# One block in eight of the scan's input multiplied by a diagonal on TensorE instead of being scaled on ScalarE and transposed

## The chip, the cores and the metric

The kernel runs on one core of one Trainium2 chip. The metric is the time on the device, in microseconds (us), of one execution; the number given for a kernel is the median of several. A core has TensorE (PE in the profile; its weight loads are PEld), VectorE (DVE), ScalarE (ACT), GpSimd (POOL), and SyncE (SP), which here issues the DMAs.

## What is computed

The network has two layers on an input of 8 images of 64 x 64 pixels with 192 channels. Layer 0 is a state space block with convolutions and an MLP; the change does not touch it. Layer 1 is a selective scan over the pixels in four directions. Cut to what matters, with L = 4096 positions, 384 inner channels, 16 states and K = 4 directions:

```python
xs = four orders of the pixels                 # (b, K, 384, L)
delta = softplus(dts + bias)                   # (b, K, 384, L)
def step(h, inp):                              # one position
    d, bm, cm, uu = inp
    h = exp(d[..., None] * A) * h + (d * uu)[..., None] * bm[:, :, None, :]
    return h, einsum('bkdn,bkn->bkd', h, cm)   # h: (b, K, 384, 16)
_, ys = scan(step, h0, (delta, B, C, xs))
```

For every channel c and state n the state h obeys h(t) = e(t) h(t-1) + g(t), with e(t) = exp(delta(c,t) A(c,n)) and g(t) = delta(c,t) u(c,t) B(n,t). The output is the sum over the 16 states of C(n,t) h(t). The four directions are added up, normalised, gated and projected.

## The kernel before

**Layout.** Layer 0 runs first for all images. Then, image by image, a `front` (input projection and convolution) and, beside it, the `finish` of the image before; their order is worked out by a small planner. Then comes `main`, the scan of the image, in which every engine keeps the order in which the code writes its instructions (`keep_in_program_order`). The scan is nearly the whole of layer 1.

**Steps and units.** A step is a direction k (0 to 3) and a chunk of 512 positions: 32 steps for an image. A step has 8 pairs p of states and 3 blocks d of 128 channels, so 24 units, numbered u = 3p + d. A unit puts two states times 64 channels on the 128 partitions, and the two halves f of its 128 channels side by side, so its tiles are 128 x 2 x 512 in fp32.

**What a unit does**, in the order of `main`:

- `run(u)`: two scans on DVE (L1634), `hs` from `ea` and `g`, one per half f. POOL then copies the last column for the next chunk (`cy`, L1646) and multiplies by C (`hc`, L1648).
- `decay(u + 2)`: two exponentials on ACT, `ea` (L1607), into one of three buffers.
- `weigh`: ACT makes the input of the scan. `duT` holds delta times u with positions on the partitions, four blocks j of 128 positions by 384 channels. For a state n, `pw` is `duT[:, j]` times B(n), a number per partition (L1592): 384 elements. Two states i = 0, 1 fill one tile `pw` per p and j, so a pair takes 8 calls, spread over three units as 3, 3 and 2. They run ten calls ahead. There are eight buffers.
- `supply(u + 1)`: PE transposes `pw` block by block (L1618), eight transposes of 128 x 128 into `g` in PSUM, with channels and states on the partitions and positions along the free axis. `g` has two buffers.
- `collect(u - 1)`: PE adds the two states of `hc` into `y` (L1663), for each half f a fp32 matmul with 64 output columns onto partitions 0 to 63 or 64 to 127. In direction 0, the first pair also adds the skip term (`dskip`, L1661).
- `add(u - 2)`: after the last pair DVE adds `y` to the image's sum.
- pieces of `prepare(s + 1)`, one or a few at fixed units: the projections of the next step on PE (`p_d` L1481 at units 2 to 4, `p_b` L1497, `p_dt` L1510 at 7, 9 and 12, `p_du` L1532), softplus on ACT, and products on DVE. They share one PSUM bank.

So PE's order is: group of transposes for unit u + 1, `collect(u - 1)`, pieces, group of unit u + 2, and so on. `ident` is the 128 x 128 identity; `bt` holds B with positions on the partitions.

Of the kernel before, what the change touches and what calls it, by code (L numbers as in the profile page):

```python
# [8 lines left out]
F32 = mybir.dt.float32  # L9
AF = mybir.ActivationFunctionType  # L10
# [18 lines left out]
NB1 = TT // 128  # L29
# [155 lines left out]
def step(engine, weight, do, after=None, table=None):  # L185
    return engine, weight, do, after, table
# [846 lines left out]
def layer1(tc, consts, x1s, mv1, out, w_in, w_x, w_dt, w_out):  # L1033
    nc = tc.nc
    ident, grp, eps, p128 = consts
# [5 lines left out]
    with ExitStack() as ctx:  # L1041
# [37 lines left out]
        for m in range(2 * DT):  # L1079
            for ct in range(CT):  # L1080
# [4 lines left out]
                    start=ct == 0,  # L1085
                    stop=ct == 1,
# [4 lines left out]
        o = lambda ins: keeper[-1](ins)  # L1091
# [343 lines left out]
        def scan(xo):  # L1435
# [5 lines left out]
            pools, ready = {}, {}  # L1441

            def spool(name, bufs, **kw):
                pools[name] = cx.enter_context(tc.tile_pool(name=name, bufs=bufs, reuse_waits="tile", **kw))
# [3 lines left out]
            state = [dict() for _ in steps]  # L1448
# [127 lines left out]
            def load_c(s, p):  # L1576
                state[s]["cb", p] = cb = pools["bc1"].tile([128, TT], F32, name="cb")
                for i in range(2):
                    o(
                        nc.sync.dma_start(  # L1580
                            out=cb[i * 64 : i * 64 + 64], in_=state[s]["cd"][2 * p + i].partition_broadcast(64)
                        )
                    )

            def weigh(s, p, j, i):

                st = state[s]
                if i == 0:
                    st["pw", p, j] = pools["pw1"].tile([128, 2 * DT, 2, 64], F32, name="pw")
                n = 2 * p + i  # L1590
                o(
                    nc.scalar.activation(  # L1592
                        st["pw", p, j][:, :, i],
                        st["duT"][:, j].rearrange("p (g c) -> p g c", c=64),
                        AF.Copy,
                        scale=st["bt"][:, j, n : n + 1],
                    )
                )

            def decay(u):  # L1600
                s, p, d = units[u]
                k, c = steps[s]
                made["e", u] = ea = pools["e1"].tile([128, 2, TT], F32, name="ea")
                for f in range(2):
                    at = 2 * d + f
                    o(
                        nc.scalar.activation(  # L1607
                            ea[:, f], state[s]["dr", d][:, f], AF.Exp, scale=an[:, k, p, at : at + 1]
                        )
                    )  # L1610

            def supply(u):
                s, p, d = units[u]
                made["g", u] = g = pools["g1"].tile([128, 2, TT], F32, name="g")
                for f in range(2):
                    for j in range(NB1):
                        o(
                            nc.tensor.transpose(  # L1618
                                g[:, f, j * 128 : j * 128 + 128],
                                state[s]["pw", p, j][:, 2 * d + f].rearrange("p a b -> p (a b)"),  # L1620
                                ident,
                            )
                        )
# [57 lines left out]
            def prologue(f, mq, front_pools):  # L1681

                yield "wait", "front"
                front_pools.close()
                for name, n in (("pr1", 2), ("dr1", 4), ("pw1", 8), ("bc1", 3), ("e1", 3)):
                    spool(name, n)
                load_first = prepare(0, lambda name: mq.tile([128, TT], F32, name=name, tag="mm"))
                ready.update({fn.__name__: fn for at in sorted(load_first) for fn, *_ in load_first[at]})
                r = yield step("SP", 0.1, ready["load"])
                yield "take", "mm"  # L1690
                r += 3.5
                for d in range(DT):
                    r = yield step("PE", 0.95, lambda: ready["project"](d), r)
                r = yield step("DVE", 0.7, ready["keep"])
                f.give("mm", r)
                f.at["xd"] = r
                yield "take", "mm"
                yield step("PE", 0.6, ready["turn_b"])
                r = yield step("DVE", 0.2, ready["keep_b"])
                f.give("mm", r)  # L1700
                f.at["bt"] = r
                load_c(0, 0)
                for d in range(DT):
                    yield "wait", ("du", d)
                for t in todo[:10]:
                    yield step("ACT", 0.55, lambda: weigh(*t), f.free["ACT"])
                for u in range(2):
                    yield step("ACT", 1.35, lambda: decay(u), None, "explog")
# [19 lines left out]
            def main():  # L1728
                for name, n, kw in (("h1", 3, {}), ("y1", 1, dict(space=PSUM)), ("g1", 2, dict(space=PSUM))):
                    spool(name, n, **kw)  # L1730
                supply(0)
                rest = iter(todo[10:])
                nu = len(units)
                for u, (s, p, d) in enumerate(units):
                    if p == 0 and d == 0:
                        pieces = prepare(s + 1) if s + 1 < len(steps) else {}
                    s2, p2 = (s, p + 1) if p < NP1 - 1 else (s + 1, 0)
                    if s2 < len(steps) and d == 0:
                        load_c(s2, p2)
                    run(u)  # L1740
                    if u + 2 < nu:
                        decay(u + 2)
                    for _ in range((3, 3, 2)[d]):
                        if t := next(rest, None):
                            weigh(*t)
                    if u + 1 < nu:
                        supply(u + 1)
                    if u >= 1:
                        collect(u - 1)
                    if u >= 2:  # L1750
                        add(u - 2)
                    for f, *args in pieces.get(p * DT + d, ()):
                        f(*args)
                collect(nu - 1)
                add(nu - 2)
                add(nu - 1)
                cx.close()

            def chains(f, mq, front_pools):
                f.pool("tmp", 2)  # L1760
                return [prologue(f, mq, front_pools)] + [prologue_of(f, d) for d in range(DT)]
# [3 lines left out]
        for b in range(nb + 1):  # L1765

            f = Flow(tc, after=True)
            f.STAY = 0.0
            keeper.append(f.keep)
            mq_x, fr_x, fi_x = ExitStack(), ExitStack(), ExitStack()  # L1770
            mq = mq_x.enter_context(tc.tile_pool(name="mq1", bufs=5, space=PSUM, reuse_waits="tile"))
            f.pool("mm", 5)
            chains = []
            if b < nb:
                xo = [ddp.tile([128, DT, L], F32, name=f"xo{i}") for i in range(2)]
                xo.append(ddp.tile([L, DIN], F32, name="xo2"))
                chains += front(f, fr_x, mq, b, xo)
                prologue, main = scan(xo)
                chains += prologue(f, mq, fr_x)
            if b:  # L1780
                chains += finish(f, fi_x, mq, b - 1)
            for gen in chains:
                f.chain(gen)
            f.run()
            fi_x.close()
            mq_x.close()
            keeper.append(tc.keep_in_program_order)
            if b < nb:
                explog(tc)
                main()  # L1790
# [103 lines left out]
```

## Time and profile before

| | |
|---|---|
| time, median of 3 runs | 23752.58 us (23742.58 to 23754.5) |
| profiled execution, its own time | 23759.13 us |
| its span | 23757.4 us |
| PE matmuls busy | 21089.6 us |
| PE weight loads busy | 10279.5 us |
| DVE busy | 21274.2 us |
| ACT busy | 21040.0 us |
| POOL busy | 16067.4 us |
| scans, L1634 (both forms) | 13024.0 + 1763.7 us |
| `hc` on POOL, L1648 | 14592.9 us, 2375 ns each |
| `pw` on ACT, L1592 | 8874.1 us, 16384 of 601 ns |
| `ea` on ACT, L1607 | 8120.5 us, 12288 of 709 ns |
| transposes, L1618 | 6788.4 us, 49152 of 279 ns |
| `y` on PE, L1663 | 6624.0 us, 24576 of 617 ns |

How to read it: busy is the time in which an engine had an instruction under way, and the mean of one instruction is from its start to its end, so neighbours overlap; for a row of instructions, the distance from start to start counts. The profile has the whole program, layer 0 too, in which POOL is little used; the scan is read from windows of it. A wait is put down to the semaphore that came last by the profile, and this can name the wrong engine. A fp32 matmul shows as two records of the same size, a transpose as one.

### The profile page before, as it was taken

To read this page: it belongs to the slowest core of one execution; us is meant where nothing else is said; L and a number is where in the kernel's file an instruction comes from. 1 tells how busy PE (TensorE), PEld (TensorE's weight loads), DVE (VectorE), ACT (ScalarE), POOL (GpSimd) and SP (SyncE) were. 2 spreads that over 40 slices of the span, in tenths; PEclk is the share of its full clock that TensorE was granted. 3 is DMA by queue.
4 is the path that set the end of the run, shared out by engine and by line. 5 is a ranking of instruction groups with operands and counts; after the bars stand their busy time and mean duration, and the time that the engine had idled before them with its cause. 6 is when DMAs were issued, how large, how long until landed. Compare 5 with 4: busy or idle time off the path is not lost.

```text
span 23757.4 us, 313126 instructions
## 1 busy us (share of the span) xinstructions
PE 21089.6 (89%) x100804; PEld 10279.5 (43%) x100804; DVE 21274.2 (90%) x22093; ACT 21040.0 (89%) x37507; POOL 16067.4 (68%) x12871
## 2 busy tenths in 40 slices
PE   7999999978888888888888888888888888888888
PEld 4444444434444444444444444444444444444444
DVE  7888888779998999899989998999899989998998
ACT  5666766669998999899989998999899989998998
POOL 1111111149995999599959985998699769976997
PEclk8999999989999999999999999999999999999999
DMA  2111111133233323333233233323332233233332
GB/s 50 45 44 44 46 44 43 39 99 81 81 79 107 81 82 78 107 81 82 76 112 81 82 77 109 81 81 79 110 82 81 78 107 82 81 85 100 82 83 67
DMA packets 1368290, 1859.75 MB, mean 78 GB/s; under 512 B 268576, under 2 KB 697024, under 8 KB 1357440
## 3 DMA queue, kind: packets, MB, share of 16 engines
q1 hardware_dynamic: 1366656, 1839.73, 28.7%
q8 instruction: 810, 13.27, 0.2%
q14 instruction: 824, 6.75, 0.1%
HBM read 1225.98 MB, written 210.50 MB: 60 GB/s over the span
## 4 chain that ended last, share of the span: by engine, by line
POOL 43%; PE 24%; ACT 15%; DVE 7%; issue 6%; DMA 4%; SPq 1%; POOLq 0%; ACTq 0%; DVEq 0%
POOL hc L1648 40%; ACT pw L1592 6%; ACT ea L1607 6%; POOL cy L1646 3%; PE p_f L956 3%; DMA xc<-xo 2%; DVE xs L1202 2%; PE p_f L976 2%; PE p_x L448 2%; PE y L1663 2%; PE p_o L873 2%; PE p_y L790 1%; PE g L1618 1%; PE p_d L1481 1%; PE p_z L531 1%
## 5 line engine op out<-in xcount | busy, mean ns | idle before, releaser
L1648 POOL TENSOR_TENSOR hc<-hs,cb 128x1024 f32<-128x1024 f32 x6144 | 14592.9, 2375 | 12.0 <-POOL cy L1646 9.9
L1634 DVE TENSOR_TENSOR_SCAN hs<-ea,cy,g 128x512 f32<-128x512 f32 x10752 | 13024.0, 1262 | 608.6 <-PE g L1618 411.1
L1592 ACT ACTIVATE pw<-duT,bt 128x384 f32<-128x384 f32 x16384 | 8874.1, 601 | 20.2 <-DVE duT L1539 20.2
L1607 ACT ACTIVATE ea<-dr,an 128x512 f32<-128x512 f32 x12288 | 8120.5, 709 | 189.2 <-DVE hs L1634 170.8
L1663 PE MATMUL y<-hc,sel 128*64 128x512 f32 x24576 | 6624.0, 617 | 1841.3 <-POOL hc L1648 1819.2
L1618 PEld LDWEIGHTS g<-ident,pw 128*128 128x128 f32 x49152 | 5288.7, 141 | 4336.8 <-issue 2671.4
L1618 PE MATMUL g<-ident,pw 128*128 128x128 f32 x49152 | 6788.4, 279 | 60.1 <-ACT pw L1592 28.6
L1646 POOL COPY cy<-hs 128x2 f32<-128x2 f32 x6144 | 1164.2, 189 | 3373.5 <-DMA out_x<-xl 1733.8
L1663 PEld LDWEIGHTS y<-hc,sel 128*64 128x64 f32 x24576 | 1225.9, 134 | 3254.1 <-POOL hc L1648 3031.3
L1634 DVE TENSOR_TENSOR_SCAN hs<-ea,g 128x512 f32<-128x512 f32 x1536 | 1763.7, 1202 | 159.0 <-PE g L1618 115.6
L365 POOL TENSOR_TENSOR s<-xs 96x512 f32<-96x512 f32 x64 | 121.1, 1892 | 2033.7 <-DVE xs L343 1522.9
L1202 DVE SCALAR_TENSOR_TENSOR xs<-pad,p,xs 128x4096 f32<-128x4096 f32 x192 | 860.9, 4484 | 43.4 <-ACT xs L1192 36.2
L1510 PE MATMUL p_dt<-xdbl,wd 13*128 13x512 f32 x1536 | 857.2, 639 | 41.0 <-DVE de L1523 39.1
L365 POOL TENSOR_TENSOR s<-sq 96x512 f32<-96x512 f32 x128 | 211.6, 1653 | 964.1 <-ACT sq L378 899.8
L1481 PE MATMUL p_d<-xc,wx 128*44 128x512 f32 x1536 | 791.6, 598 | 22.6 <-DMA xc<-xo 22.0
L343 DVE SCALAR_TENSOR_TENSOR x<-xx,p,x 96x512 f32<-96x512 f32 x1024 | 785.2, 815 | 19.4 <-ACT x L332 19.4
L956 PE MATMUL p_f<-h,wf 96*128 96x512 f32 x1536 | 761.9, 632 | 24.4 <-ACT zs L550 14.0
L343 DVE SCALAR_TENSOR_TENSOR xs<-xin,p,xs 96x512 f32<-96x512 f32 x1024 | 749.3, 767 | 4.6 <-ACT xs L332 4.6
L976 PE MATMUL p_f<-m,wf 128*96 128x512 f32 x1536 | 692.9, 601 | 0.0
L1532 PEld LDWEIGHTS p_du<-ident,de 128*128 128x128 f32 x3072 | 323.5, 141 | 610.2 <-DVE de L1523 405.8
L448 PE MATMUL p_x<-h,wi 96*128 96x512 f32 x1024 | 544.5, 664 | 12.3 <-ACT h L405 11.1
L365 POOL TENSOR_TENSOR s<-x 96x512 f32<-96x512 f32 x64 | 96.2, 1502 | 626.3 <-DVE x L343 477.2
(202 smaller groups left out, 19557.2 us busy)
## 6 DMA issues: line engine op xcount, KB each, us to landing
cb<-cd SPq DMA_DIRECT2D x4096, 128.0 KB
dr<-de SPq DMA_DIRECT2D x3072, 128.0 KB
xc<-xo SPq DMA_DIRECT2D x256, 768.0 KB
e<-csd SPq DMA_DIRECT2D x256, 384.0 KB
xl<-x SPq DMA_DIRECT2D x256, 384.0 KB
ut<-xo SPq DMA_DIRECT2D x128, 768.0 KB
ut<-xo SPq DMA_DIRECT2D x256, 384.0 KB
xo<-xs SPq DMA_DIRECT2D x48, 1024.0 KB
```

What stands on the lines that cost most here:

```text
L343: nc.vector.scalar_tensor_tensor(im(out[:, ct]), tap(ct, j), w[:, ct, j : j + 1], im(out[:, ct]), ALU.mult, ALU.add)
L956: nc.tensor.matmul(ps, wf1[:, ct, mt * 128 : mt * 128 + 128], h[:, ct], start=ct == 0, stop=ct == 1)
L976: nc.tensor.matmul(ps[:CP], wf2[:, kt, ct * CP : ct * CP + CP], m[:, kt], start=kt == 0, stop=kt == 5)
L1202: nc.vector.scalar_tensor_tensor(xs, tap(j), kw[:, d, j : j + 1], xs, ALU.mult, ALU.add)
L1481: nc.tensor.matmul(st["p_d"][:44], wx[:, d, k], st["xc"][:, d], start=d == 0, stop=d == DT - 1)
L1592: nc.scalar.activation(st["pw", p, j][:, :, i], st["duT"][:, j].rearrange("p (g c) -> p g c", c=64), AF.Copy, scale=st["bt"][:, j, n : n + 1],
L1607: nc.scalar.activation(ea[:, f], state[s]["dr", d][:, f], AF.Exp, scale=an[:, k, p, at : at + 1])
L1618: nc.tensor.transpose(g[:, f, j * 128 : j * 128 + 128], state[s]["pw", p, j][:, 2 * d + f].rearrange("p a b -> p (a b)"), ident,)
L1634: nc.vector.tensor_tensor_scan(rev(h[:, f]), rev(ea[:, f]), rev(g[:, f]), 0.0 if first(s) else state[s - 1]["cy"][:, p, d, f : f + 1], ALU ...
L1646: o(nc.gpsimd.tensor_copy(st["cy"][:, p, d], h[:, :, last]))
L1648: o(nc.gpsimd.tensor_mul(hc, h, bc(st["cb", p], 1, [128, 2, TT])))
L1663: o(nc.tensor.matmul(y[half[f]], sel, hc[:, f], start=p == 0 and k > 0, stop=p == NP1 - 1))
```

## The change

In the odd pairs p, block j = 3 (the last of four) is made in another way. `weigh` no longer multiplies the 384 channels of `duT` by B(n). It writes B(n) on a diagonal: `bd[:, i]` is the identity times B(n), 128 elements per partition, one tile `bd` with both states, two buffers. `supply` then does not transpose this block. For each half f and each state i a matmul takes 64 channels of `duT` as weights and the diagonal as the moving operand, onto partitions 0 to 63 or 64 to 127 of `g`; the product with a diagonal scales each position by its B and turns the block at the same time. For an odd unit, two of eight transposes become four matmuls. The pool of `pw` tiles has seven buffers instead of eight, since two pairs now make seven such tiles.

```diff
+            def diagonal(p, j):
+                return p % 2 == 1 and j == NB1 - 1
+
             def weigh(s, p, j, i):
                 st = state[s]
+                if diagonal(p, j):
+                    if i == 0:
+                        st["bd", p, j] = pools["pw1"].tile([128, 2, 128], F32, name="bd", bufs=2)
+                    n = 2 * p + i
+                    o(nc.scalar.activation(st["bd", p, j][:, i], ident, AF.Copy, scale=st["bt"][:, j, n : n + 1]))
+                    return
                 if i == 0:
                     st["pw", p, j] = pools["pw1"].tile([128, 2 * DT, 2, 64], F32, name="pw")
...
             def supply(u):
...
                 for f in range(2):
                     for j in range(NB1):
+                        if diagonal(p, j):
+                            at = (2 * d + f) * 64
+                            for i in range(2):
+                                o(
+                                    nc.tensor.matmul(
+                                        g[i * 64 : i * 64 + 64, f, j * 128 : j * 128 + 128],
+                                        state[s]["duT"][:, j, at : at + 64],
+                                        state[s]["bd", p, j][:, i],
+                                        start=True,
+                                        stop=True,
+                                    )
+                                )
+                            continue
                         o(
                             nc.tensor.transpose(
...
-                for name, n in (("pr1", 2), ("dr1", 4), ("pw1", 8), ("bc1", 3), ("e1", 3)):
+                for name, n in (("pr1", 2), ("dr1", 4), ("pw1", 7), ("bc1", 3), ("e1", 3)):
```

## The prediction

> **What bounds the kernel now.** I read the busy shares first, then the busy time of one step of the scan, then who waited for whom, then the timeline of a few units. Units are numbered u = 3p + d inside a step (24 units), a step is one direction and one chunk of 512 tokens; 8 images x 32 steps = 256 steps.
>
> The page: busy shares, and the chain by engine.
> ```profile
> PE 21089.6 (89%) x100804; PEld 10279.5 (43%) x100804; DVE 21274.2 (90%) x22093; ACT 21040.0 (89%) x37507; POOL 16067.4 (68%) x12871
> POOL 43%; PE 24%; ACT 15%; DVE 7%; issue 6%; DMA 4%; SPq 1%; POOLq 0%; ACTq 0%; DVEq 0%
> ```
> Three engines are level, and the chain is mostly POOL and PE. Next, the busy times of two whole steps of one image, one of direction 1 and one of direction 0 (columns: length, then PE, PEld, DVE, ACT, POOL).
> ```profile
> 12851.09:12916.64 65.55, 57.79 (x318) 28.47 (x316) 63.19 (x60) 65.38 (x120) 59.89 (x49) 1.00 0.32 83
> 12256.83:12323.28 66.45, 60.12 (x330) 29.17 (x329) 63.10 (x60) 65.31 (x119) 59.91 (x49) 1.00 0.27 74
> ```
> ACT is busy 65.38 of 65.55 us, so it looks like the bound. But the second step has the same ACT work and takes 0.9 longer: something else can set the length. The waits over 1,700 us of one scan (us, times, longest):
> ```profile
> DVE hs L1634 <- PE g L1618: 53.7, 82, 1.3
> PE y L1663 <- POOL hc L1648: 184.8, 352, 1.1
> PE g L1618 <- ACT pw L1592: 2.3, 10, 0.3
> ACT ea L1607 <- DVE hs L1634: 5.1, 8, 1.1
> ```
> DVE waits for PE's `g`, PE for POOL's `hc`, POOL for DVE's scan; PE almost never stands still for ACT's `pw`; ACT's only waits are for DVE. The timeline of unit 9 shows the loop (start, length, engine, work, idle before):
> ```profile
> 12870.79 2.38 POOL L1648 TENSOR_TENSOR hc<-hs,cb 128x1024 f32<-128x1024 f32 x1
> 12873.22 1.08 PE L1663 MATMUL y<-hc,sel 128*64 128x512 f32 x4 [0.53 <-POOL hc L1648]
> 12874.23 1.12 PE L1510 MATMUL p_dt<-xdbl,wd 13*128 13x512 f32 x2
> 12875.28 1.09 PE L1618 MATMUL g<-ident,pw 128*128 128x128 f32 x8
> 12876.30 1.08 PE L1663 MATMUL y<-hc,sel 128*64 128x512 f32 x4
> 12877.31 1.09 PE L1618 MATMUL g<-ident,pw 128*128 128x128 f32 x8
> 12876.51 2.45 DVE L1634 TENSOR_TENSOR_SCAN hs<-ea,cy,g 128x512 f32<-128x512 f32 x2 [1.14 <-PE g L1618]
> ```
> `hc` of unit 6 ends at 12873.17; then PE runs without a gap: `y`, `p_dt`, the transposes of unit 9 (end 12876.37), and 0.14 later the scan starts. It waits for all eight transposes, as `g` is one tile. The same at units 4 and 5, of the direction 1 step and of the direction 0 step, where PE has the extra `dskip` matmuls:
> ```profile
> 12862.22 2.45 DVE L1634 TENSOR_TENSOR_SCAN hs<-ea,cy,g 128x512 f32<-128x512 f32 x2 [0.44 <-ACT pw L1592]
> 12865.16 2.45 DVE L1634 TENSOR_TENSOR_SCAN hs<-ea,cy,g 128x512 f32<-128x512 f32 x2 [0.49 <-PE g L1618]
> ...
> 12266.91 1.08 PE L1661 MATMUL y<-xc,dskip 128*64 128x512 f32 x4
> 12267.82 1.03 PE L1663 MATMUL y<-hc,sel 128*64 128x512 f32 x4
> 12269.63 1.09 PE L1618 MATMUL g<-ident,pw 128*128 128x128 f32 x8
> 12270.86 2.45 DVE L1634 TENSOR_TENSOR_SCAN hs<-ea,cy,g 128x512 f32<-128x512 f32 x2 [1.29 <-ACT ea L1607]
> ```
> The releasers "ACT" are wrong here: each of these scans starts 0.14 after its last transpose ends (12269.63 + 1.09 = 12270.72). The 0.9 us of extra PE work turns a wait of 0.49 into 1.29 and the step from 65.5 into 66.5. So the loop DVE, POOL, PE sets the pace; ACT runs beside it with 0.2 us to spare per step.
>
> **The skill.** "TensorEngine Tiling (Array Packing)", Key Properties: changing the tiling mode drains TensorE. The trace agrees: `y` (64 columns) to `p_d` (44 columns) takes 0.91 from start to start, `y` to `g` (128 columns) 1.01, so a change costs 0.10. "FP8 and Floating Point Precision", TensorE Precision Notes: true fp32 takes four passes. Here a 512-column fp32 matmul is two records of 0.43 (`p_d` x2 takes 0.95 with a drain), while a 128-column transpose is one record of 0.11. "ScalarE: Activation LUTs", What ACT_TABLE_LOAD costs: 0.833 ns per element. In the timeline three `pw` of 384 take 1.52 and two `ea` of 512 take 1.23, which is 0.108 per 128 elements; it agrees.
>
> **The change, part by part.** Per step, four odd pairs.
>
> ACT: 8 ACTIVATEs go from 384 elements (0.51) to 128 (0.51 - 0.22 = 0.29): 1.7 us less per step, 63.7 of work. Worth 1.7 x 256 = 440 us if ACT set the pace; by the reading above, about nothing.
>
> PE, in the 12 odd units of a step: 2 of 8 transposes go (2 x 0.11), and 4 matmuls of 64 x 128 columns come, each in two records. Like the two halves of `y`, the pair for i = 0, 1 writes different partition halves, and `y`'s four records go in two rounds, so I take two rounds of 0.107 per pair. The order per f is three transposes, then the pair: the mode changes three times more inside the group. A change costs 0.10 drain plus 0.05 for a weight load that nothing hides (eight transposes take 1.02 to the next `y`: 0.05 + 8 x 0.109 + 0.10). Before, from the first start: 0.05 + 7 x 0.109 = 0.82 to the last start. After: transposes 0.05 + 0.33 + 0.10 = 0.48, pair 0.05 + 0.21 + 0.10 = 0.36, transposes 0.48, pair 0.05 + 0.107 to its last round: 1.48. **The group ends 0.66 later.** The following `y` is in the pair's mode and saves one change, so PE's queue grows by 0.51. Bounds: with no cost of changes 2 x 0.214 - 2 x 0.109 = +0.21; with the two halves one after the other 0.66 + 2 x 0.214 = +1.09. No gain is possible, since two rounds are longer than one transpose. I take 0.66, because each term is a row of this trace.
>
> At nothing: `pw` keeps its reuse distance (8 tiles per two pairs before, 7 now), `bd`'s two buffers come round after four pairs. If that were wrong, ACT would wait, and it has 3 us to spare then. PE's wait for `pw` becomes one for `bd`, which ACT finishes earlier than before; behind it queue `collect` and the pieces of `prepare`, as now. No DMA, DVE or POOL instruction changes.
>
> Where 0.66 lands, walked along the timeline of the direction 1 step; slack is the time from a group's end to its scan, less 0.14. Unit 3 has 0.61: +0.05. Unit 4 has none: its group (12860.99 to 12862.08) ends at 12862.74, +0.66. PE is free for the next `y` 1.59 after the group's start, at 12862.58 instead of 12862.07; with 0.86 for `y` and 0.95 for `p_d` the group of unit 5 starts at 12864.39, lasts 1.75, and its scan starts at 12866.28 instead of 12865.16: +1.1, and all that follows in DVE's order with it. Unit 9, into which PE runs without a gap: 1.1 + 0.66, +1.8. Unit 10 has 0.9 of slack: still +1.8. Unit 11: group 9 (from 12876.40), `y`, group 10, `y`, `p_dt` and group 11 now run back to back, 1.59 + 0.96 + 1.59 + 0.96 + 1.05 + 1.75, to 12884.30, and the scan that started at 12881.85 starts at 12884.44: +2.6. Units 15 to 17 have slacks of 0.5 to 0.8, which hold 0.66 but for +0.1. Units 21 to 23 have none, but PE stands 0.36 before each `y`, which takes up most of the 0.51: +0.66, then +0.1 in all. Sum **+3.5 us per step**. In direction 0 the `dskip` matmuls of unit 1, which run now while PE waits for `hc`, find no such gap behind the longer group of unit 3: unit 4 +1.2 and unit 5 +1.7, so +4.1 for the step.
>
> Sum: 8 images x (8 x 4.1 + 24 x 3.5) = 934 us. Front, finish and layer 0 do not change. The profiled execution took 23759.1 (span 23757.4), so about 24,690; the median 23752.6 is 6 us lower, within rounding.
>
> **Rivals.**
> (1) ACT is the bound after all: 440 us less, 23,310. For it: 65.38 of 65.55 busy. Against: ACT itself waits for DVE, the direction 0 step is longer at equal ACT work, and after the change the group of transposes must fit where no slack is left. It decides from the point where the group gets no longer at all, since units 4, 5, 9 and 21 have no slack, and only if the last thing those scans wait for is ACT's. Chance 0.06.
> (2) Changes of mode cost little when weights are loaded ahead: +0.21 to +0.40 per group. The same walk gives 0.9 to 1.8 per step, 23,990 to 24,240. For it: PE can load weights early. Against: every change in the trace costs 0.10 or more. Chance 0.09.
> (3) The two halves do not overlap (+1.09): about 6.2 per step, 25,350. For it: 128 columns is short. Against: `y`'s rounds. Chance 0.05.
> (4) ACT's relief and PE's cost cancel, within 0.2%: 23,750. It needs both bounds to be loose; chance 0.02.
>
> **How the numbers follow.** The main case, +0.4 to +0.9 per group, has 0.78: 24,240 to 25,050. Its point is 24,690. Slack that PE finds in POOL's jitter, or in a cheaper change of mode, lowers it more easily than anything raises it, so the range for 8 in 10 reaches from 24,150 to 25,050; it takes in part of (2) and leaves (1), (3) and (4) out. Faster by over 0.2% (what a measurement of this kernel can tell from no change, 47 us): 0.06, from (1). Same: 0.02. Slower: 0.92.
>
> **What would show it.** In the changed profile: a row of `g<-bd,duT` matmuls with 128-column operands, two rounds about 0.11 apart, groups of an odd unit 1.7 to 1.8 long instead of 1.09; `pw` 14336 times and 2048 short ACTIVATEs of about 0.38; ACT's share falling, with ACT waiting about 5 us per step for the scan; DVE's wait for `g` rising from 2.4 to about 5.9 per step, with new waits at units 5, 9, 11 and 21. It is wrong if odd groups last under 1.4, or if a scan with a longer group starts no later than now, or if ACT stays without waits.

## The result and the profile after

The changed kernel takes 24,691 us (24,677 to 24,711) against 23,753 (23,743 to 23,755): ratio 1.0395, 95% interval 1.0382 to 1.0407. The prediction was 24,690. The scans of the eight images are 115 to 118 us longer each (in the mean 2100 before and 2217 after, from the first scan instruction to the last), which is 938 of the 941 us between the two spans; all that lies outside the scans is as it was, to 4 us.

The page of the changed kernel: busy shares, the chain by engine, and five of the costliest groups (busy, mean ns of one, then idle of the engine before them and its releaser).
```profile
PE 22618.6 (92%) x119236; PEld 10836.1 (44%) x119236; DVE 21326.1 (86%) x22093; ACT 20987.2 (85%) x37507; POOL 16135.7 (65%) x12871
POOL 41%; PE 30%; DVE 11%; issue 7%; ACT 6%; DMA 5%; SPq 0%; POOLq 0%; DVEq 0%; ACTq 0%
L1657 DVE TENSOR_TENSOR_SCAN hs<-ea,cy,g 128x512 f32<-128x512 f32 x10752 | 13062.3, 1263 | 1386.7 <-PE g L1631 1269.1
L1617 ACT ACTIVATE ea<-dr,an 128x512 f32<-128x512 f32 x12288 | 8183.9, 713 | 1144.5 <-DVE hs L1657 1050.5
L1641 PE MATMUL g<-ident,pw 128*128 128x128 f32 x43008 | 6673.3, 284 | 16.5 <-DVE hs L1657 12.5
L1631 PE MATMUL g<-bd,duT 128*64 128x128 f32 x24576 | 2701.3, 298 | 0.0
L1596 ACT ACTIVATE bd<-ident,bt 128x128 f32<-128x128 f32 x2048 | 696.2, 388 | 0.0
```
The work of DVE and POOL is the same; PE has 1,530 us more of it. The idle time of DVE before its scans went from 609 to 1,387 us, and what ends it is now the new matmul, L1631. ACT's idle time before `ea` went from 189 to 1,145 us: it waits for DVE.

The same two steps as before the change, one of direction 1 and one of direction 0 (length, then PE, PEld, DVE, ACT, POOL busy).
```profile
13316.37:13385.66 69.29, 63.65 (x390) 30.61 (x388) 63.50 (x60) 65.19 (x119) 60.32 (x49) 1.00 0.30 77
12687.14:12757.75 70.61, 66.19 (x402) 31.41 (x400) 63.43 (x61) 65.19 (x119) 60.24 (x49) 1.00 0.27 76
```
65.55 became 69.29 (+3.7), and 66.45 became 70.61 (+4.2). PE and its weight loads are busier; the other engines gain at most 0.4 us of busy time. The timeline of units 4 and 5 of the direction 1 step, PE and then DVE (start, length, work, idle before):
```profile
13325.31 1.02 PE L1481 MATMUL p_d<-xc,wx 128*44 128x512 f32 x2
13326.26 0.55 PE L1641 MATMUL g<-ident,pw 128*128 128x128 f32 x3
13326.74 0.44 PE L1631 MATMUL g<-bd,duT 128*64 128x128 f32 x4
13327.11 0.55 PE L1641 MATMUL g<-ident,pw 128*128 128x128 f32 x3
13327.58 0.44 PE L1631 MATMUL g<-bd,duT 128*64 128x128 f32 x4
13327.85 1.03 PE L1686 MATMUL y<-hc,sel 128*64 128x512 f32 x4
...
13328.17 2.45 DVE L1657 TENSOR_TENSOR_SCAN hs<-ea,cy,g 128x512 f32<-128x512 f32 x2 [1.01 <-PE g L1631]
13331.57 2.45 DVE L1657 TENSOR_TENSOR_SCAN hs<-ea,cy,g 128x512 f32<-128x512 f32 x2 [0.95 <-PE g L1631]
```
Read the starts: transposes 0.48, pair 0.37, transposes 0.47, pair 0.27 to the next `y`, 1.59 in all where it was 1.08. The last matmul ends at 13328.02, 1.76 after the group began, and the scan starts 0.15 later. The waits over 1,700 us of one scan (us, times, longest; from 12753 to 14453, so that no pause between two images is in it) have grown on DVE's and ACT's side:
```profile
DVE hs L1657 <- PE g L1631: 137.7, 123, 1.9
ACT ea L1617 <- DVE hs L1657: 91.0, 174, 1.9
PE y L1686 <- POOL hc L1671: 120.5, 247, 1.2
```
DVE's wait for PE was 53.7, ACT's for DVE 5.1, PE's for POOL 184.8: PE has used up part of its own waits and passed the rest on to DVE.

### The profile page after: what moved, and what is told of

The parts are those of the page before. It is cut to its first block, busy times and chain, and to the rows that moved or that the text cites. A ratio compares the mean times of both kernels' runs of the same rounds, so it can differ in the third digit from the quotient of the medians.

```text
span 24698.7 us, 349990 instructions
## 1 busy us (share of the span) xinstructions
PE 22618.6 (92%) x119236; PEld 10836.1 (44%) x119236; DVE 21326.1 (86%) x22093; ACT 20987.2 (85%) x37507; POOL 16135.7 (65%) x12871
## 4 chain that ended last, share of the span: by engine, by line
POOL 41%; PE 30%; DVE 11%; issue 7%; ACT 6%; DMA 5%; SPq 0%; POOLq 0%; DVEq 0%; ACTq 0%
POOL hc L1671 38%; DVE hs L1657 4%; PE y L1686 4%; PE g L1641 4%; POOL cy L1669 3%; PE p_f L956 2%; PE p_dt L1510 2%; ACT ea L1617 2%; DVE xs L1202 2%; PE g L1631 2%; DMA ut<-xo 2%; PE p_f L976 2%; PE p_x L448 2%; ACT pw L1602 2%; PE p_o L873 1%
## 5 line engine op out<-in xcount | busy, mean ns | idle before, releaser
L1602 ACT ACTIVATE pw<-duT,bt 128x384 f32<-128x384 f32 x14336 | 7843.0, 602 | 18.4 <-DVE duT L1539 18.4
L1686 PE MATMUL y<-hc,sel 128*64 128x512 f32 x24576 | 6514.9, 608 | 1304.7 <-POOL hc L1671 1249.6
L1641 PE MATMUL g<-ident,pw 128*128 128x128 f32 x43008 | 6673.3, 284 | 16.5 <-DVE hs L1657 12.5
L1641 PEld LDWEIGHTS g<-ident,pw 128*128 128x128 f32 x43008 | 4571.9, 141 | 4693.2 <-issue 2242.0
L1631 PE MATMUL g<-bd,duT 128*64 128x128 f32 x24576 | 2701.3, 298 | 0.0
L1686 PEld LDWEIGHTS y<-hc,sel 128*64 128x64 f32 x24576 | 1349.9, 135 | 2281.6 <-POOL hc L1671 2175.4
L1631 PEld LDWEIGHTS g<-bd,duT 128*64 128x64 f32 x24576 | 1216.7, 135 | 1029.9 <-issue 983.7
L1596 ACT ACTIVATE bd<-ident,bt 128x128 f32<-128x128 f32 x2048 | 696.2, 388 | 0.0
```

The costliest lines, as they stand in the source:

```text
L1602: nc.scalar.activation(st["pw", p, j][:, :, i], st["duT"][:, j].rearrange("p (g c) -> p g c", c=64), AF.Copy, scale=st["bt"][:, j, n : n + 1],
L1631: nc.tensor.matmul(g[i * 64 : i * 64 + 64, f, j * 128 : j * 128 + 128], state[s]["duT"][:, j, at : at + 64], state[s]["bd", p, j][:, i], s ...
L1641: nc.tensor.transpose(g[:, f, j * 128 : j * 128 + 128], state[s]["pw", p, j][:, 2 * d + f].rearrange("p a b -> p (a b)"), ident,)
L1686: o(nc.tensor.matmul(y[half[f]], sel, hc[:, f], start=p == 0 and k > 0, stop=p == NP1 - 1))
```

## The experiments

The theory: the loop DVE, POOL, PE sets the pace of the scan; a longer group on PE costs time where no slack stands before its scan; the group's length is two rounds per pair plus the changes of mode. (A round is the time of one record of a matmul, or of two that write different halves of the partitions side by side. Transposes write 128 columns, `y`, `p_d` and the diagonal's matmuls 64 or fewer; going from the one kind to the other is a change of mode.) The rivals: ACT is the bound; the loss has another source (the wait for the diagonal, the pool); changes of mode are free; a group costs the same wherever it stands. Each comparison below is with runs of the kernel before on the same chip (23,746 to 23,763 in the median).

### Each half of the change alone

`e1_act_only`: `weigh` as in the change, `supply` with eight transposes.
```diff
-                                state[s]["pw", p, j][:, 2 * d + f].rearrange("p a b -> p (a b)"),
+                                state[s]["pw", p, j - diagonal(p, j)][:, 2 * d + f].rearrange("p a b -> p (a b)"),
```


> The ScalarE half of the change alone: it writes the diagonal (128 elements) and not the 384, and TensorE makes eight transposes as before, with block 2 taken a second time in place of block 3 (so block 3 of odd pairs is left out of the computation). Loop theory (DVE, POOL, PE set the pace): no change, 23,700 to 23,760, with ACT now waiting 1.7 us per step more. Rival, ACT is the bound: 440 us less, 23,310.

`e2_pe_only`: `weigh` as before, `supply` as in the change with `ident` for `bd`, eight `pw` buffers.
```diff
-                                        state[s]["bd", p, j][:, i],
+                                        ident,
```


> The TensorE half alone: ScalarE makes all eight 384-element products of a pair as before, TensorE makes the four small matmuls with the plain identity as moving operand (so B is left out of block 3 of odd pairs). Loop theory: all of the loss is here, 24,650 to 24,730. Rival, part of the loss comes from the wait for the diagonal or the smaller pool: clearly below 24,690. Rival, ScalarE's relief gave something back in the changed kernel: up to 25,130.

Measured: `e1_act_only` 23,698, ratio 0.9975 (0.9964 to 0.9986). `e2_pe_only` 24,687, ratio 1.0388 (1.0372 to 1.0404). The whole loss is in the TensorE half, and neither the wait for `bd` nor the pool has a part in it: with them gone and with ACT's old work back, the time is that of the changed kernel. ACT's relief alone is worth 60 us and not 440 (2 us below the range that the theory gave; a small gain, but a real one). A direction 1 step of `e1_act_only`, and its waits over 1,700 us:
```profile
12887.00:12952.53 65.53, 57.38 (x318) 28.52 (x316) 63.18 (x61) 63.98 (x120) 59.97 (x49) 1.00 0.31 78
```
```profile
ACT ea L1617 <- DVE hs L1644: 32.1, 70, 1.1
```
ACT is busy 1.4 us less, and the step is as long as before to 0.02 us; ACT waits for DVE, 32.1 us instead of 5.1. Where the 60 us are, step by step from the two traces, whose spans differ by 55: the first step of each direction is 0.9 us shorter (32 such steps, 29 us in all), the other steps of direction 0 together 11 us, and the last step of each image 1.0 (8 us in all). The other 160 steps are equal; their sum differs by less than 1 us. A first step of direction 1, before and in `e1_act_only`:
```profile
12654.99:12720.02 65.03, 58.14 (x318) 28.42 (x316) 60.55 (x60) 64.93 (x119) 60.01 (x49) 1.00 0.30 77
12626.25:12690.34 64.09, 57.34 (x318) 28.46 (x316) 60.58 (x60) 62.98 (x118) 59.82 (x49) 1.00 0.31 77
```
In the first steps the scans are shorter (the form without `cy`, 1.20 instead of 1.26 us), and with less work of ACT the step gets shorter, as the steady ones do not: there ACT was the last. So the rival holds for about one step in eight. In direction 0 the gain is at unit 4, whose scan starts 0.15 earlier; its cause is open. The remaining 7 us lie ahead of the first scan; over the traces kept here that scan starts anywhere from 5,038 to 5,075 us, although layer 0 is the same in all of them, so this is no effect of the change.

### What makes the group longer

`e3_one_mode`: the kernel before, a full fp32 matmul instead of a transpose for block 3 of odd pairs.
```diff
+                        if p % 2 == 1 and j == NB1 - 1:
+                            o(nc.tensor.matmul(out, block, ident, start=True, stop=True))
+                        else:
+                            o(nc.tensor.transpose(out, block, ident))
```


> The kernel before, with block 3 of odd pairs turned by a full fp32 matmul with the identity (128 columns, two records) and not by a transpose: the second round is paid as in the change, but no mode changes. Theory with the terms of the prediction: +0.22 per group, by the walk +1.1 us per step, 24,045. Rival, the rounds are what costs and mode changes are free: as slow as the changed kernel, 24,690.

`e7_matmuls_last`: the changed kernel, with the blocks in the order T T T T T T M M.
```diff
-                for f in range(2):
-                    for j in range(NB1):
+                for f, j in sorted(((f, j) for f in range(2) for j in range(NB1)), key=lambda at: diagonal(p, at[1])):
```


> The changed kernel with the six transposes of an odd unit first and the four matmuls after them: one more mode change in the group instead of three. Theory: the group ends 0.36 later than before and not 0.66, PE's queue grows by 0.2: +1.6 us per step, 24,175. Rival, mode changes are free: 24,690, as the changed kernel.

Measured: `e3_one_mode` 24,009, ratio 1.0101 (1.0083 to 1.0119). `e7_matmuls_last` 24,144, ratio 1.0159 (1.0142 to 1.0175). PE's timeline at unit 4, first of `e3_one_mode` (L1620 are the matmuls, two records each), then of `e7_matmuls_last`:
```profile
13040.99 0.55 PE L1622 MATMUL g<-ident,pw 128*128 128x128 f32 x3
13041.37 0.39 PE L1620 MATMUL g<-ident,pw 128*128 128x128 f32 x2
13041.59 0.49 PE L1622 MATMUL g<-ident,pw 128*128 128x128 f32 x3
13041.92 0.39 PE L1620 MATMUL g<-ident,pw 128*128 128x128 f32 x2
13042.24 1.08 PE L1662 MATMUL y<-hc,sel 128*64 128x512 f32 x4
```
```profile
13065.30 0.88 PE L1641 MATMUL g<-ident,pw 128*128 128x128 f32 x6
13066.11 0.66 PE L1631 MATMUL g<-bd,duT 128*64 128x128 f32 x8
13066.59 1.03 PE L1686 MATMUL y<-hc,sel 128*64 128x512 f32 x4
```
In one mode, three transposes take 0.38 (after a change) and 0.33, the matmul between them 0.22, and the group 1.25 to the next `y`; where `y` followed at once, the eight transposes took 1.02. The 0.23 are the two extra records. With the matmuls together at the end there is one more change instead of three and the group takes 1.29; spread out it takes 1.59. Both kernels do as many rounds as the changed one, and are 680 and 550 us faster than it (36 and 31 us below what was expected of them). Of the loss of 938 us, some 250 are the second round. The 550 go with two of the three changes of mode, as `e7_matmuls_last` differs from the changed kernel in nothing but the order. The last 135 go with the third change or with the matmuls being half as wide; no run takes these two apart. Free changes of mode are ruled out.

### Where the group stands

The change in one pair only; `pw` with eight buffers.
```diff
-                return p % 2 == 1 and j == NB1 - 1
+                return p == 5 and j == NB1 - 1
```


> The change in pair 5 alone (units 15 to 17), a quarter of it, where the walk finds slack of 0.5 to 0.8 before each scan. Theory: the slack holds the 0.66, +0.1 to +0.2 us per step, 23,780 to 23,810. Rival, every group costs the same share of the loss, wherever it stands: a quarter of 938, 23,990.

The same with `p == 1`:

> The change in pair 1 alone (units 3 to 5), where units 4 and 5 have no slack and PE also does p_d. Theory: +1.15 us per step, +1.6 in direction 0, 24,075. Rival, the same share everywhere: 23,990.

Measured: `e4_pair5` 23,771, ratio 1.0009 (1.0003 to 1.0016). `e5_pair1` 24,046, ratio 1.0123 (1.0108 to 1.0139). The same three groups cost 25 us in one place and 300 in another (9 us below the expected range, and 29 below the expected point). In the trace of `e4_pair5` the scan of unit 17 starts 0.2 later than before, relative to its step, and no other adds to that; in `e5_pair1` the shift is 0.68 at unit 4, 1.14 at unit 5 and 1.13 at the end of the step (1.03, 1.55 and 1.54 in direction 0; medians over the steps of a direction but its first and last). The place decides. The 25 us are a balance: in directions 1 to 3 the steps but the first lose 35 us together, and the first steps gain 12, as they did in `e1_act_only`.

### Half of the wait taken away

`g` as two tiles, one for each half, in the same banks:
```diff
-                made["g", u] = g = pools["g1"].tile([128, 2, TT], F32, name="g")
+                made["g", u] = g = [pools["g1"].tile([128, TT], F32, name=f"g{f}") for f in range(2)]
```
On the kernel before:

> The kernel before with g as two tiles, one per half, so that the first scan of a unit waits for four transposes and not for eight (0.44 us earlier). Loop theory: DVE's stalls at units 4, 9 and 21 fall by 0.4 each; then ACT, 65.4 us of work in a step, is the next bound: 23,640 to 23,700, most of the gain in direction 0. Rival, ACT is the bound already: no change in directions 1 to 3 and in direction 0, 23,753.

On the changed kernel:

> The changed kernel with g as two tiles. The first half of an odd unit is then ready 0.84 us earlier than in the changed kernel, before the point of the kernel before, while PE's queue still carries 0.51 more per odd unit. Theory (wait and queue both count): most of the loss goes, a part stays where PE runs without a gap (units 5, 11), about +0.7 us per step, 23,850 to 23,980. Rival, only the wait for the end of the group counts: the stalls are gone and ACT's relief shows, 23,400 to 23,500.

Measured: `e6_before_two_tiles` 23,661, ratio 0.9966 (0.9953 to 0.9979). `e8_after_two_tiles` 23,943, ratio 1.0081 (1.0066 to 1.0096). DVE and a step of `e6_before_two_tiles`, units 9 to 15:
```profile
12897.31 2.45 DVE L1634 TENSOR_TENSOR_SCAN hs<-ea,cy,g 128x512 f32<-128x512 f32 x2 [0.67 <-PE g L1618]
12899.68 0.66 DVE L1523 SCALAR_TENSOR_TENSOR de<-spa,p_dt 128x512 f32<-128x512 f32 x1
12900.26 4.79 DVE L1634 TENSOR_TENSOR_SCAN hs<-ea,cy,g 128x512 f32<-128x512 f32 x4
12905.55 0.69 DVE L1523 SCALAR_TENSOR_TENSOR de<-spa,p_dt 128x512 f32<-128x512 f32 x1 [0.51 <-ACT spa L1518]
```
```profile
12872.83:12938.06 65.23, 58.44 (x318) 28.42 (x317) 63.04 (x61) 65.14 (x119) 59.76 (x50) 1.00 0.31 80
```
The stall at unit 9 is 0.67 instead of 1.14, and in directions 1 to 3 those at units 4 and 21 are gone (in direction 0 the one at unit 4 is not: 0.82 instead of 0.59). In their place DVE waits for ACT's softplus, `spa`, twice a step. ACT is busy 65.14 of 65.23: here it is the bound, and the step cannot get shorter than ACT's work. That is the second limit that the loop had hidden, 0.3 us below it. In `e8_after_two_tiles`, where ACT has less work, DVE shows what is left of PE's queue:
```profile
12984.23 2.45 DVE L1657 TENSOR_TENSOR_SCAN hs<-ea,cy,g 128x512 f32<-128x512 f32 x2 [0.28 <-POOL hc L1671]
12987.63 2.45 DVE L1657 TENSOR_TENSOR_SCAN hs<-ea,cy,g 128x512 f32<-128x512 f32 x2 [0.95 <-PE g L1631]
12998.97 2.45 DVE L1657 TENSOR_TENSOR_SCAN hs<-ea,cy,g 128x512 f32<-128x512 f32 x2 [0.96 <-PE g L1631]
13005.12 1.28 DVE L1657 TENSOR_TENSOR_SCAN hs<-ea,cy,g 128x512 f32<-128x512 f32 x1 [0.76 <-PE g L1631]
```
These are units 4, 5, 9 and 11. At 4 and 9, where the wait for the end of the group counted, 0.7 to 0.9 has gone (1.01 to 0.28, 1.82 to 0.96). At 5 and 11, which stand behind an unbroken run of PE, the stall is what it was in the changed kernel, 0.95 and 0.76. So both parts of the walk are real: the end of a group, and PE's queue.

### A version that beats both

With the two tiles, a diagonal where there is slack, and an order of blocks in which the matmuls stand next to the `y` before and after them (M TTT TTT M: two changes of mode for `y` and group together, as before), and eight `pw` buffers:
```diff
+                if diagonal(p, NB1 - 1):
+                    blocks = [(0, 3), (0, 0), (0, 1), (0, 2), (1, 0), (1, 1), (1, 2), (1, 3)]
...
-                return p % 2 == 1 and j == NB1 - 1
+                return p in (4, 5, 6) and j == NB1 - 1
```


> The version that the readings point to: g as two tiles, the diagonal in pairs 4, 5 and 6 only (where there is slack), and in an odd order of blocks, so that the mode changes twice in a group and not more often than around it before: matmuls of half 0, three transposes, three transposes, matmuls of half 1. ACT has 1.3 us less per step (64.1), PE's queue 0.2 more per such unit. Theory: ACT was the bound after g was split, so now the loop with its stalls at units 5 and 9 is, 64.3 to 64.5 us per step and 65.3 in direction 0: 23,440 to 23,520. Rival, ACT's relief is worth nothing also then: 23,660, as with the two tiles alone.

The same order and tiles with all odd pairs, and seven buffers:

> The same two tiles and order of blocks with the diagonal in all odd pairs, as in the changed kernel. Theory: half 0 is ready 0.33 earlier than in the kernel before, PE's queue is 0.2 longer per odd unit, so units 5 and 11 take back most of it: about 0.2 us less per step than before, 23,680 to 23,740, slower than with pairs 4 to 6. Rival, the order alone makes the change pay in every pair: 23,440 or less.

Measured: `e9_two_tiles_pairs456` 23,479, ratio 0.9883 (0.9866 to 0.9899). `e10_all_odd_mttm` 23,613, ratio 0.9937 (0.9922 to 0.9951). The second is 70 us under the range expected. Expected were half 0 ready 0.33 earlier than before, most of it taken back by units 5 and 11, and about 0.2 us less per step. Measured against the kernel before in direction 1, the scan of unit 4 starts 0.33 earlier, unit 5 0.17 and unit 9 0.32 earlier, and unit 11 0.02 later; so far it is as expected. But units 14 and 21 then gain another 0.16 and 0.30, and the step ends 0.49 earlier. The walk had left these two out, although the two tiles alone give them: in `e6_before_two_tiles` they gain 0.16 and 0.26.

Neither has the gain that ACT's smaller work would allow. In the first, DVE stalls before unit 14, which it did not before:
```profile
12806.05 1.12 PE L1510 MATMUL p_dt<-xdbl,wd 13*128 13x512 f32 x2
12807.10 0.44 PE L1634 MATMUL g<-bd,duT 128*64 128x128 f32 x4
12807.47 0.88 PE L1644 MATMUL g<-ident,pw 128*128 128x128 f32 x6
...
12808.16 2.45 DVE L1660 TENSOR_TENSOR_SCAN hs<-ea,cy,g 128x512 f32<-128x512 f32 x2 [0.50 <-PE g L1644]
```
Unit 14 is in pair 4, and `p_dt` stands right before its group. Pair 0 in place of pair 4:

> As the version with pairs 4, 5 and 6, with pair 0 in place of pair 4: pair 4 showed a stall of 0.5 us before unit 14 that no other pair has, and pair 0 stands where VectorE has extra work of the step before. Theory (the place of a group decides): the 0.5 goes, ACT's work stays the same, 0.4 to 0.5 us less per step, 23,350 to 23,400. Rival, the share of blocks decides and not the place: 23,479 as with pairs 4, 5 and 6.

Measured: 23,370, ratio 0.9839 (0.9823 to 0.9856). At the same place DVE runs through, and a step takes 63.97:
```profile
12786.12 4.78 DVE L1660 TENSOR_TENSOR_SCAN hs<-ea,cy,g 128x512 f32<-128x512 f32 x4
```
```profile
12750.46:12814.43 63.97, 60.71 (x372) 31.00 (x374) 62.80 (x61) 63.87 (x119) 59.75 (x49) 1.00 0.32 84
```
The same work on every engine as with pair 4, 109 us less. ACT's relief of the change is worth its 1.3 us per step once the loop does not stand in front of it: 65.23 with two tiles alone, 63.97 here.

## Why the prediction was right, and where not

**The bound.** Right. The loop DVE, POOL, PE set the pace and ACT was close behind; `e1_act_only` shows it from one side, `e6_before_two_tiles` from the other. In the changed kernel ACT's relief is worth nothing, as predicted: `e2_pe_only` has none and is as slow to 4 us. On its own it is worth 60 us, half of them from the first step of each direction, which the prediction had not looked at.

**The length of a group.** Right: 1.59 to the next `y` and 1.76 to the end, predicted 1.59 and 1.75. The terms hold one by one: the second round (0.23 for the two of a group in `e3_one_mode`, reckoned 0.21) and a change of mode (0.15 in `e7_matmuls_last`, reckoned 0.15).

**The walk.** Right, to about 0.2 us at every unit. Shift of the scan's start in direction 1, predicted and measured (medians over the steps of the direction but its first and last): unit 3 0.05 and 0.00; unit 4 0.66 and 0.68; unit 5 1.1 and 1.15; unit 9 1.8 and 1.82; unit 11 2.6 and 2.61; after unit 17 2.7 and 2.85; end of the step 3.5 and 3.72. Direction 0: unit 4 1.2 and 1.03, unit 5 1.7 and 1.55, end 4.1 and 4.11 (the same excess later on makes up for what units 4 and 5 lack). The small excess of direction 1 is at unit 17 (0.1 was given for units 15 to 17, 0.24 measured) and at units 21 to 23 (0.76 given, 0.87 measured); over all steps of directions 1 to 3 but the first it is 21 us. The total is nevertheless right, because the first step of each direction, which the walk did not treat apart, moved by 3.0 to 3.3 and not by 3.5 to 4.1: 17 us less. The two misses cancel, and the agreement to 1 us is luck.

**ACT's busy time.** Wrong in a detail: I expected ACT busy 63.7 per step, and it is 65.19. The short ACTIVATEs do cost 0.29 from start to start. But busy time counts an instruction to its end, and ACT now stands still after 17 instructions of a step and not after 5 (means of directions 1 to 3, without first and last steps). The Trainium skill says ("ScalarE: Activation LUTs", What ACT_TABLE_LOAD costs) that back-to-back ACTIVATEs overlap by about 93 ns; here `bd` lasts 0.388 and the next one starts after 0.292, an overlap of 0.096. Where ACT stands still, the overlap is lost and shows as busy time: 12 times 0.096 is 1.2 us. In the same steps each of the 48 `ea` lasts 6 ns longer, 0.3 us; the two make up the 1.5 that were missed. I had named ACT's waiting as about 5 us per step; it is 3.7 (91.0 over 24.5 steps). DVE's wait for `g` is 5.6 (137.7 over 24.5), predicted about 5.9. The sign and the place were right.

**The rivals.** ACT as the bound is out for about seven steps in eight. That its relief cancels PE's cost is out by `e2_pe_only`. Cheap changes of mode are out by `e3_one_mode` and `e7_matmuls_last`. That the halves do not overlap is out by the records: four in two rounds, 0.27 to the next `y`.

What stays open: what the 135 us between `e3_one_mode` and `e7_matmuls_last` are made of, and why `e1_act_only` gains 11 us in the steady steps of direction 0.

## What to carry to other kernels

An engine that is busy 99% of a stage need not be its bound: look whether it ever waits for the others, and compare two stages in which its work is equal and their lengths are not. When work moves from one engine to another, price it by the time from start to start, with each change of mode in it, and then follow it unit by unit through the waits; the same extra cost 25 us in one place and 300 in another. Before moving work off the busiest engine, shorten the wait that the loop stands on (here: one tile made into two), or the relief cannot show.

## What the runs showed of the hardware

Half-width fp32 matmuls on different halves of the partitions run side by side also when the moving operand has only 128 columns: four records take 0.27 us to the next matmul of the same mode (the changed kernel), eight take 0.48 (`e7_matmuls_last`), which is 0.05 and two or four rounds of 0.107. A change of mode cost 0.15 in the group: with two fewer it took 1.29 instead of 1.59. Two parts of it show apart. From `y` to `p_d`, without a change, 0.91 pass, and from `y` to `g`, with one, 1.01: 0.10 for leaving the old mode. And `y` behind a matmul of its own mode takes 0.86 to `p_d` instead of 0.91: 0.05 for arriving, which I read as the first weight load, which nothing hides then. So two changes cost nearly as much as three transposes of 0.11, and here it paid to put matmuls of one mode side by side, although that changed the order of the output blocks.
